# A state-space mixer, a feed-forward and linear attention on one core: y turned by feature tile from a buffer of its own, decay computed in place in four tiles, diagonals by chunk

## The chip, the cores and the metric

The kernel runs on one core of a Trainium2 chip. The core has a matrix engine (TensorE, PE in the profile, its weight loads PEld), a vector engine (VectorE, DVE), an activation engine (ScalarE, ACT), a general engine (GpSimd, POOL) and a queue processor (SyncE, SP). Each works through its own queue in order, and they wait for each other at semaphores. Tiles lie in an on-chip memory of 128 partitions (SBUF), matmul results in eight PSUM banks of 128 x 512 fp32 values. The metric is device time in microseconds of one execution.

## The reference

For 16 sequences of 512 tokens with 256 features the program computes four blocks, each with a layer norm in front and a residual add behind:

```python
x = x + mamba(layernorm(x), ...)      # L0_attn_a
x = x + ffn(layernorm(x), ...)        # "f"
x = x + attention(layernorm(x), ...)  # L0_attn_b, linear, causal, 16 heads
x = x + ffn(layernorm(x), ...)        # "g", same weights
```

The first block is a scan over time with 16 states per feature:

```python
x_in = x @ w_in;  dt_low, Bm, Cm = split(x_in @ w_x)
dt = softplus(dt_low @ w_dt + b_dt) * 0.099 + 0.001
A = -exp(A_log)
# at each token, for every feature d and state n:
h = exp(dt[d] * A[d, n]) * h + inp_term[n]     # inp_term sums dt * A * u over d, times Bm
y[d] = sum_n h[d, n] * Cm[n] + Dp[d] * x_in[d]
```

The feed-forward quantizes its inputs, its weights and its hidden layer to 4-bit floats in blocks of 16 and dequantizes them again: `fp4_linear(silu(fp4_linear(x, w_gate)) * fp4_linear(x, w_up), w_down)`. All is in fp32.

## The kernel before

A sequence b is one tile x of 128 x 4 x 256 (token in a chunk, chunk c, feature), which stays on the chip through all four blocks.

**Prologue** (`front`, L430, and `prologue`, L444). Mean and variance by `bn_stats` (L437), 1/sigma on GpSimd (L391). `to_features` (L408) turns x to 2 feature tiles of 128 x 512: for a layer norm it makes four diagonal matrices of 1/sigma (L414, one tile "diag" of four chunks with a single buffer) and multiplies each 128x128 piece of x by its diagonal on TensorE (L421), first the four chunks of feature tile k = 0 in one PSUM bank, then those of k = 1 in another, with a copy (L425) after each. From this come pz, tile "soft" (Abs, Tanh and Ln, L461 to L467), dt (L468, the last read of "soft"), which goes to DRAM as dd in eight DMAs (L473), C as cm (L478), u (L485) and the input term (L497).

**Mamba** (L501) has 16 steps, by feature half e (2), group j (4) and pair q0 (2). A step takes 16 features by two groups of eight, with the 16 states of eight features on 128 partitions.
- `spread` (L508) loads dt of these features from dd by DMA into a tile sp, 128 x 2 x 512, each row repeated for 16 states. sp has three buffers, and the load is asked for two steps ahead.
- `decay` (L518) computes bar = exp(dt A) as the square of the Exp of half the exponent: two Exp (L524) from sp into one of two constant tiles bar, then one Square in place (L527). It is written one step ahead of its scan. Column 0 of each bar stays zero, so that the scan starts anew there.
- A scan over 2 x 512 elements (L545) into h (three buffers), a product with cm (L549), and after every second step four matmuls (eight instructions, L555) that sum over the states into py. py is a single PSUM bank of its own pool (128 x 512, all of one half e); the half opens with a matmul by the diagonal of Dp (two instructions, L541) and ends with a copy to yT (L562).
- yT holds both halves (128 x 2 x 512) and has the tag "soft", with one buffer: it takes turns with the prologue's "soft" tile.
- When both halves are there, yT is turned back in eight 128x128 transposes (L571) into two banks, and `residual` (L374) adds each chunk of 128x256 to x on VectorE with its row sum (L377), followed by a Square on ScalarE that accumulates the squared distances from the mean (L381). These sums feed the next layer norm.

**Feed-forward** (`ffn`, L578) quantizes the normalized x, turns it, and then for each of the four chunks does gate and up matmuls (L599), silu (L605 to L607), quantization (L226 to L252), turning (L621, copied to hqT by L625) and the down matmul po (L634). **Attention** (L656) turns x with its 1/sigma by `to_features`, makes q and k (L671 to L679), and by chunk scores (four banks psc, masked to sm by L722), numerator and denominator, and the projection (L793).

Seven PSUM banks (pool `ps`, L73) serve all of this except py. A tile's buffer goes to the next tile of the same tag, in program order, when its last reader is done.

**Order.** The blocks are Python generators that yield weights; `weave` (L834) puts a piece of the next sequence's prologue after each step of mamba, and `by_turns` (L874) advances two generators in proportion to their weights. For sequence b the loop at L897 runs two such stages: mamba(b) with prologue(b+1) and the start of f(b) beside g(b−2) and the front of attention(b−1), then the chunks of f(b) beside the rest of attention(b−1). `some(new, FIRST)` cuts the first stage at a weight of 74. This is the order in which instructions are written. The framework then sets the order on each engine itself: earlier-written work goes first, and later work is taken up where it is ready and the engine would be free. In the trace, early scans of mamba(b) therefore stand between instructions of f(b−1) and attention(b−2).

Of the kernel before, what the change touches and what calls it, by code (L numbers as in the profile page):

```python
# [17 lines left out]
P = 128  # L18
# [14 lines left out]
def kernel(  # L33
# [31 lines left out]
    NBAR = 2  # L65
    NSP = 3
# [91 lines left out]
    for t in vpads:  # L158
        nc.gpsimd.memset(t, 0.0)

# [213 lines left out]
    def residual(xt, c, add, stats):  # L374
# [5 lines left out]
        )  # L380
        nc.scalar.activation(  # L381
# [26 lines left out]
    def to_features(pool, t, name, rstd=None):  # L408

        tT = pool.tile([P, ND, S], F32, tag="tT", name=f"tT_{name}", bufs=1)  # L410
        if rstd is not None:
            diag = small.tile([P, NC, P], F32, tag="diag", name=f"diag_{name}", bufs=1)
            for c in range(NC):
                nc.scalar.activation(diag[:, c, :], ident, AF.Copy, scale=rstd[:, c : c + 1])  # L414
        for k in range(ND):
            pt = bank(f"pt_{name}_{k}")
            for c in range(NC):
                if rstd is None:
                    nc.tensor.transpose(pt[:, ts(c, P)], t[:, c, ts(k, P)], ident)
                else:  # L420
                    nc.tensor.matmul(  # L421
                        pt[:, ts(c, P)], t[:, c, ts(k, P)], diag[:, c, :],
                        start=True, stop=True,
                    )
            nc.scalar.copy(tT[:, k, :], pt)  # L425
        return tT
# [74 lines left out]
    def mamba(b, xt):  # L501
# [5 lines left out]

        def spread(e, j, q0):  # L508

            sp = one.tile([P, 2, S], F32, tag="sp", name=f"sp_{b}_{e}_{j}_{q0}", bufs=NSP)  # L510
            src = dd[e, q0 // 2, j * G8 : (j + 1) * G8].rearrange("i q t -> i (q t)")
            nc.sync.dma_start(
                sp.rearrange("p q t -> p (q t)"),
                src.unsqueeze(0).to_broadcast([NS, G8, 2 * S]),
            )
            return sp

        def decay(sp, e, j, q0):  # L518

            bar = bars[state["bar"] % NBAR]  # L520
            state["bar"] += 1
            for i in range(2):
                g = 16 * e + 4 * (q0 + i) + j
                nc.scalar.activation(  # L524
                    bar[:, i, 1:S], sp[:, i, 1:S], AF.Exp, scale=a_col[:, g : g + 1]
# [5 lines left out]
        sps = [spread(*steps[at]) for at in range(NSP - 1)]  # L531
        ahead = decay(sps[0], *steps[0])
        for at, (e, j, q0) in enumerate(steps):
            bar = ahead
            if at + NSP - 1 < len(steps):
                sps.append(spread(*steps[at + NSP - 1]))
            if at + 1 < len(steps):
                ahead = decay(sps[at + 1], *steps[at + 1])
            if j == 0 and q0 == 0:
# [398 lines left out]
```

## Time and profile before

| | |
|---|---|
| median of 3 runs | 3023.27 us (3021.46 to 3023.94) |
| the profiled execution | 3014.09 us, span 3012.4 us |
| busy: TensorE, VectorE, ScalarE, GpSimd | 82%, 81%, 50%, 5% of the span |
| mean granted TensorE clock | 0.915 |
| L545 scans, 256 | 581.0 us, 2281 ns each |
| L549 products, 256 | 308.5 us, 1208 ns each |
| L524 Exps, 512 | 352.1 us, 716 ns each; idle before them 392.0 us |
| L527 Squares, 256 | 269.1 us, 1051 ns each |
| DMA of sp, 256 of 512 KB | 4.6 us to landing |

The profile is of one execution; times in views are microseconds from the span's start. A line of instructions gives its start, duration, engine, line of the kernel, operation and tiles (out<-in), and in brackets how long the engine had been idle and what ended that. A line of waits gives who waited for whom, the total, how many times, and the longest. The chain lists the work that ended last, step by step. Busy matmul time is modelled, so a full TensorE is not TensorE at its peak. From the fourth sequence on the first scans (L545) of sequences follow each other at 177.4 to 181 us.

### The profile page before, as it was taken

The numbers are of one execution on the slowest core, as the hardware profiler recorded it, in microseconds if no ns is written. First come the engines' busy times: TensorE is split into PE (matmuls) and PEld (weight loads), VectorE is DVE, ScalarE is ACT, GpSimd is POOL, SyncE is SP. The second block draws the span as 40 slices with busy tenths as digits, with TensorE's granted clock in tenths as the row PEclk, the third lists the DMA queues.
The fourth block names the chain that finished last, engine by engine and source line by source line (L and its number), as shares of the span: only waits on it lengthen the run. The fifth ranks groups of instructions, "written<-read, shape, count | busy, mean of one in ns | idle before, by whom it ended". The sixth has DMA issues, their size and how long they took to land.

```text
span 3012.4 us, 34256 instructions
## 1 busy us (share of the span) xinstructions
PE 2463.3 (82%) x12907; PEld 1464.3 (49%) x12907; DVE 2451.0 (81%) x3545; ACT 1507.3 (50%) x2846; POOL 144.7 (5%) x169
## 2 busy tenths in 40 slices
PE   6576898979888797888979788787878879787897
PEld 3142544545455454545545454454545545454654
DVE  7969679697897969889796987979698787987565
ACT  5746264554545555454555546455554645543222
POOL 2000000000000000000000000000000000000000
PEclk8787897998999899999999999899999989998988
DMA  5513012031231313112131311213122120310000
GB/s 140 133 42 98 21 44 76 22 91 36 54 80 29 79 34 91 36 49 77 32 80 36 83 44 49 70 28 84 37 78 54 46 74 22 84 35 1 8 1 14
DMA packets 64377, 165.27 MB, mean 55 GB/s; under 512 B 8434, under 2 KB 26836, under 8 KB 64212
## 3 DMA queue, kind: packets, MB, share of 16 engines
q1 hardware_dynamic: 62592, 162.03, 20.6%
q8 instruction: 101, 1.65, 0.2%
q10 hardware_dynamic: 1620, 1.06, 0.1%
q14 instruction: 64, 0.52, 0.1%
HBM read 146.28 MB, written 16.78 MB: 54 GB/s over the span
## 4 chain that ended last, share of the span: by engine, by line
DVE 49%; PE 31%; ACT 10%; issue 6%; POOL 2%; DMA 0%; DVEq 0%; SPq 0%; ACTq 0%; POOLq 0%
DVE h L545 13%; PE po_f L634 7%; DVE h L549 4%; PE pg_f L599 3%; PE pu_f L599 3%; PE po_g L634 3%; DVE sm L722 2%; DVE v_g L250 2%; DVE v_f L250 2%; DVE v_f L251 2%; DVE v_f L244 2%; DVE v_g L251 2%; PE pz L452 2%; PE py L555 2%; DVE h_g L252 1%
## 5 line engine op out<-in xcount | busy, mean ns | idle before, releaser
L545 DVE TENSOR_TENSOR_SCAN h<-bar,inp 128x1024 f32<-128x1024 f32 x256 | 581.0, 2281 | 7.7 <-ACT bar L527 3.3
L524 ACT ACTIVATE bar<-sp,a_col 128x511 f32<-128x511 f32 x512 | 352.1, 716 | 392.0 <-DVE h L545 384.5
L555 PE MATMUL py<-h,red 128*32 128x512 f32 x1024 | 280.8, 691 | 155.7 <-DVE h L549 155.7
L549 DVE TENSOR_TENSOR h<-h,cm 128x1024 f32<-128x1024 f32 x256 | 308.5, 1208 | 1.3
L634 PE MATMUL po_f<-wdT,hqT_f 128*128 128x256 f32 (+1 forms) x768 | 220.4, 434 | 68.6 <-ACT hqT_f L625 68.6
L527 ACT ACTIVATE bar<-bar 128x1022 f32<-128x1022 f32 x256 | 269.1, 1051 | 4.4
L634 PE MATMUL po_g<-wdT,hqT_g 128*128 128x256 f32 (+1 forms) x768 | 208.8, 416 | 22.5 <-ACT hqT_g L625 22.5
L634 PEld LDWEIGHTS po_f<-wdT,hqT_f 128*128 128x128 f32 (+1 forms) x768 | 152.7, 213 | 139.7 <-ACT hqT_f L625 93.1
L634 PEld LDWEIGHTS po_g<-wdT,hqT_g 128*128 128x128 f32 (+1 forms) x768 | 145.0, 202 | 96.7 <-ACT hqT_g L625 36.9
L599 PE MATMUL pg_f<-wgT,tT_f 128*128 128x352 f32 x512 | 182.1, 479 | 0.2 <-ACT tT_f L425 0.2
L599 PE MATMUL pg_g<-wgT,tT_g 128*128 128x352 f32 x512 | 179.1, 472 | 0.1
L679 DVE SCALAR_TENSOR_TENSOR qk<-ep 128x512 f32<-128x512 f32 x64 | 44.0, 688 | 164.1 <-ACT ep L678 164.1
L599 PE MATMUL pu_g<-wuT,tT_g 128*128 128x352 f32 x512 | 177.1, 464 | 0.0
L599 PE MATMUL pu_f<-wuT,tT_f 128*128 128x352 f32 x512 | 173.4, 461 | 0.0
L722 DVE TENSOR_TENSOR sm<-psc,causal 128x512 f32<-128x512 f32 x256 | 161.9, 679 | 13.3 <-PE psc L715 9.0
L621 PE MATMUL pt_h_g<-ident,h_g 128*128 128x128 f32 (+1 forms) x384 | 69.7, 322 | 117.8 <-DVE h_g L252 117.8
L555 PEld LDWEIGHTS py<-h,red 128*32 128x32 f32 x1024 | 35.3, 113 | 264.3 <-DVE h L549 210.0
L248 ACT ACTIVATE big_f<-v_f 128x704 bf16<-128x704 f32 (+1 forms) x80 | 67.2, 840 | 146.1 <-DVE v_f L244 146.1
L599 PEld LDWEIGHTS pg_g<-wgT,tT_g 128*128 128x128 f32 x512 | 95.3, 192 | 80.2 <-issue 41.4
L621 PEld LDWEIGHTS pt_h_g<-ident,h_g 128*128 128x128 f32 (+1 forms) x384 | 47.6, 155 | 178.3 <-DVE h_g L252 141.6
L606 DVE SCALAR_TENSOR_TENSOR h_f<-h_f,pg_f 128x352 f32<-128x352 f32 x128 | 66.1, 517 | 76.8 <-ACT h_f L605 76.8
L599 PEld LDWEIGHTS pu_g<-wuT,tT_g 128*128 128x128 f32 x512 | 97.1, 192 | 63.3 <-issue 12.6
(236 smaller groups left out, 4814.8 us busy)
## 6 DMA issues: line engine op xcount, KB each, us to landing
sp<-dd SPq DMA_DIRECT2D x256, 512.0 KB, 4.6
x<-in_L_attn_a_x_dram SPq DMA_DIRECT2D x16, 512.0 KB, 4.3
dd<-dt SPq DMA_DIRECT2D x128, 64.0 KB, 1.7
out_dram<-x SPq DMA_DIRECT2D x16, 512.0 KB, 3.5
w_qkv_sb<-in_L_attn_b_W_attn_dram ACTq DMA_DIRECT2D x1, 768.0 KB, 7.1
raw_d<-in_L_ffn_w_down_dram SPq DMA_DIRECT2D x1, 704.0 KB
raw_g<-in_L_ffn_w_gate_dram SPq DMA_DIRECT2D x1, 640.0 KB, 7.0
raw_u<-in_L_ffn_w_up_dram SPq DMA_DIRECT2D x1, 640.0 KB, 6.2
```

What stands on the lines that cost most here:

```text
L248: nc.scalar.activation(big, v, AF.Abs, scale=STEP)
L250: nc.vector.scalar_tensor_tensor(v, big, FLOOR, v, ALU.max, ALU.subtract)
L251: nc.vector.scalar_tensor_tensor(v, big, FLOOR, v, ALU.max, ALU.subtract)
L524: nc.scalar.activation(bar[:, i, 1:S], sp[:, i, 1:S], AF.Exp, scale=a_col[:, g : g + 1])
L527: nc.scalar.activation(bar[:, :, 1:S], bar[:, :, 1:S], AF.Square)
L545: nc.vector.tensor_tensor_scan(h.rearrange("p i t -> p (i t)"), bar.rearrange("p i t -> p (i t)"), inp.rearrange("p i t -> p (i t)"), 0.0, ...
L549: nc.vector.tensor_tensor(h, h, cm.unsqueeze(1).to_broadcast([P, 2, S]), ALU.mult)
L555: nc.tensor.matmul(py[32 * q : 32 * q + 32, :], red[:, j, :], (h0, h)[q // 2][:, q % 2, :], start=False, stop=(j == 3),)
L599: nc.tensor.matmul(pw[:, :HF], xqT[:, k, ts(c, P)], wT[:, k, cols], start=(k == 0), stop=(k == ND - 1),)
L621: nc.tensor.transpose(pt[:rows, ts(r - r0, P)], h[:, r * P : r * P + rows], ident)
L634: nc.tensor.matmul(po[:, :D], hqT[:rows, r, :], wdT[:rows, r, :], start=(r == 0), stop=(r == NR - 1),)
L722: nc.vector.tensor_tensor(t, psc[g].rearrange("p (s t) -> p s t", t=P), causal.unsqueeze(1).to_broadcast([P, NH // 4, P]), ALU.mult,)
```

## The change

- **y by feature tile.** At the end of each half e, py is copied to a tile yT of 128 x 512 that has a tag and a buffer of its own. Its four 128x128 pieces are turned into one bank and added to the feature half of x at once, on VectorE, as four instructions of 128x128 with partial row sums in `halves`. After the second half the two partial sums are added (128 x 4), and the four Squares follow (`distances`, split off from `residual`). The end of mamba yields 2 in place of 1.7.
- **Decay in place.** There are four bar tiles in place of two, and no sp. `spread` loads dt straight into bar, without column 0 (511 elements per row, two rows per partition), and Exp works in place. The load for step at + 3 is written after the decay of step at + 1, before the scan of step at.
- **Diagonals by chunk.** `to_features` with 1/sigma makes one 128x128 diagonal per chunk (tag "diag", two buffers, the pool's default) and uses it for both feature tiles, so two banks are filled side by side and copied at the end.

```diff
--- before.py
+++ after.py
@@ -62,8 +62,7 @@
     HF = FF // 2
     HB = P // HD
     G8 = P // NS
-    NBAR = 2
-    NSP = 3
+    NBAR = 4
     NV = 2
     NSM = 6
     DT_MIN, DT_MAX = 0.001, 0.1
@@ -378,6 +378,9 @@
             xt[:, c, :], add, 1.0, xt[:, c, :], ALU.mult, ALU.add,
             accum_out=sums[:, c : c + 1],
         )
+        distances(xt, c, sums, dist)
+
+    def distances(xt, c, sums, dist):
         nc.scalar.activation(
             squares, xt[:, c, :], AF.Square, bias=sums[:, c : c + 1], scale=-float(D),
             accum_out=dist[:, c : c + 1],
@@ -408,21 +411,23 @@
     def to_features(pool, t, name, rstd=None):
 
         tT = pool.tile([P, ND, S], F32, tag="tT", name=f"tT_{name}", bufs=1)
-        if rstd is not None:
-            diag = small.tile([P, NC, P], F32, tag="diag", name=f"diag_{name}", bufs=1)
-            for c in range(NC):
-                nc.scalar.activation(diag[:, c, :], ident, AF.Copy, scale=rstd[:, c : c + 1])
+        if rstd is None:
+            for k in range(ND):
+                pt = bank(f"pt_{name}_{k}")
+                for c in range(NC):
+                    nc.tensor.transpose(pt[:, ts(c, P)], t[:, c, ts(k, P)], ident)
+                nc.scalar.copy(tT[:, k, :], pt)
+            return tT
+        pts = [bank(f"pt_{name}_{k}") for k in range(ND)]
+        for c in range(NC):
+            diag = small.tile([P, P], F32, tag="diag", name=f"diag_{name}_{c}")
+            nc.scalar.activation(diag, ident, AF.Copy, scale=rstd[:, c : c + 1])
+            for k in range(ND):
+                nc.tensor.matmul(
+                    pts[k][:, ts(c, P)], t[:, c, ts(k, P)], diag, start=True, stop=True
+                )
         for k in range(ND):
-            pt = bank(f"pt_{name}_{k}")
-            for c in range(NC):
-                if rstd is None:
-                    nc.tensor.transpose(pt[:, ts(c, P)], t[:, c, ts(k, P)], ident)
-                else:
-                    nc.tensor.matmul(
-                        pt[:, ts(c, P)], t[:, c, ts(k, P)], diag[:, c, :],
-                        start=True, stop=True,
-                    )
-            nc.scalar.copy(tT[:, k, :], pt)
+            nc.scalar.copy(tT[:, k, :], pts[k])
         return tT
 
 
@@ -505,37 +510,35 @@
         nc.scalar.copy(inp[:, 0, :], term)
         nc.gpsimd.tensor_copy(inp[:, 1, :], term)
 
+        halves = small.tile([P, ND, NC], F32, tag="halves", name=f"halves_{b}")
+
         def spread(e, j, q0):
-
-            sp = one.tile([P, 2, S], F32, tag="sp", name=f"sp_{b}_{e}_{j}_{q0}", bufs=NSP)
-            src = dd[e, q0 // 2, j * G8 : (j + 1) * G8].rearrange("i q t -> i (q t)")
-            nc.sync.dma_start(
-                sp.rearrange("p q t -> p (q t)"),
-                src.unsqueeze(0).to_broadcast([NS, G8, 2 * S]),
-            )
-            return sp
-
-        def decay(sp, e, j, q0):
 
             bar = bars[state["bar"] % NBAR]
             state["bar"] += 1
+            src = dd[e, q0 // 2, j * G8 : (j + 1) * G8, :, 1:S]
+            nc.sync.dma_start(bar[:, :, 1:S], src.unsqueeze(0).to_broadcast([NS, G8, 2, S - 1]))
+            return bar
+
+        def decay(bar, e, j, q0):
+
             for i in range(2):
                 g = 16 * e + 4 * (q0 + i) + j
                 nc.scalar.activation(
-                    bar[:, i, 1:S], sp[:, i, 1:S], AF.Exp, scale=a_col[:, g : g + 1]
+                    bar[:, i, 1:S], bar[:, i, 1:S], AF.Exp, scale=a_col[:, g : g + 1]
                 )
             nc.scalar.activation(bar[:, :, 1:S], bar[:, :, 1:S], AF.Square)
             return bar
 
         steps = [(e, j, q0) for e in range(ND) for j in range(4) for q0 in (0, 2)]
-        sps = [spread(*steps[at]) for at in range(NSP - 1)]
+        sps = [spread(*steps[at]) for at in range(NBAR - 1)]
         ahead = decay(sps[0], *steps[0])
         for at, (e, j, q0) in enumerate(steps):
             bar = ahead
-            if at + NSP - 1 < len(steps):
-                sps.append(spread(*steps[at + NSP - 1]))
             if at + 1 < len(steps):
                 ahead = decay(sps[at + 1], *steps[at + 1])
+            if at + NBAR - 1 < len(steps):
+                sps.append(spread(*steps[at + NBAR - 1]))
             if j == 0 and q0 == 0:
                 py = ps_y.tile([P, S], F32, tag="y", name=f"py_{b}_{e}")
                 nc.tensor.matmul(py, d_diag[:, e], u[:, e, :], start=True, stop=False)
@@ -557,23 +560,25 @@
                         start=False, stop=(j == 3),
                     )
             if j == 3 and q0 == 2:
-                if e == 0:
-                    yT = one.tile([P, ND, S], F32, tag="soft", name=f"yT_{b}")
-                nc.scalar.copy(yT[:, e, :], py)
+
+                yT = one.tile([P, S], F32, tag="yT", name=f"yT_{b}_{e}")
+                nc.scalar.copy(yT, py)
+                pt = bank(f"pt_y_{b}_{e}")
+                for c in range(NC):
+                    nc.tensor.transpose(pt[:, ts(c, P)], yT[:, ts(c, P)], ident)
+                for c in range(NC):
+                    xc = xt[:, c, ts(e, P)]
+                    nc.vector.scalar_tensor_tensor(
+                        xc, pt[:, ts(c, P)], 1.0, xc, ALU.mult, ALU.add,
+                        accum_out=halves[:, e, c : c + 1],
+                    )
             yield 3.5
 
-
-        stats["f", b] = summed(0, f"f{b}")
-        for c in range(0, NC, 2):
-            pt = bank(f"pt_y_{b}_{c}")
-            for i in range(2):
-                for e in range(ND):
-                    nc.tensor.transpose(
-                        pt[:, ts(i * ND + e, P)], yT[:, e, ts(c + i, P)], ident
-                    )
-            for i in range(2):
-                residual(xt, c + i, pt[:, ts(i, D)], stats["f", b])
-        yield 1.7
+        stats["f", b] = sums, dist = summed(0, f"f{b}")
+        nc.vector.tensor_tensor(sums, halves[:, 0, :], halves[:, 1, :], ALU.add)
+        for c in range(NC):
+            distances(xt, c, sums, dist)
+        yield 2
 
     def ffn(i, nm, b, xt):
         act = acts[i]
```

## The prediction

> **What bounds the kernel now.** I read first the page's busy times, then a window view of one period, then the timeline where one engine stands idle, then waits and chain.
>
> ```profile
> PE 2463.3 (82%) x12907; PEld 1464.3 (49%) x12907; DVE 2451.0 (81%) x3545; ACT 1507.3 (50%) x2846; POOL 144.7 (5%) x169
> ```
>
> VectorE (DVE) and TensorE (PE) stand level at about four fifths, so an average cannot say which of them limits. The scans of a sequence (L545) come round every 177.4 us in the middle of the run; one such period in three windows (span, then busy time and count of each engine), then L545 alone (busy time and count on VectorE):
>
> ```profile
> core 0: us, PE busy (x) PEld busy (x) DVE busy (x) ACT busy (x) POOL busy (x), PEclk, DMA share, GB/s
> 1161.20:1233.20 72.00, 51.67 (x316) 32.58 (x316) 69.75 (x102) 36.26 (x70) 3.59 (x4) 0.88 0.31 81
> 1233.20:1311.20 78.00, 72.70 (x398) 44.30 (x398) 53.75 (x89) 40.68 (x81) 3.78 (x4) 1.00 0.11 28
> 1311.20:1338.60 27.40, 23.11 (x91) 11.43 (x89) 26.92 (x30) 16.09 (x27) 0.61 (x1) 1.00 0.29 77
> ```
>
> ```profile
> 1161.20:1251.20 90.00, 23.43 (x11) 0.91 0.29 76
> 1251.20:1312.20 61.00, 1.47 (x1) 1.00 0.07 19
> 1312.20:1338.60 26.40, 11.40 (x5) 1.00 0.30 79
> ```
>
> The first window is VectorE's (2.3 us idle of 72), the second TensorE's (5.3 idle of 78, while VectorE idles 24.3), the third VectorE's again (0.5 idle). And no scan starts for 61 us in the middle: eleven of sixteen run early, five wait until 1312. What holds them is in the timeline:
>
> ```profile
> 1293.80 1.23 DVE L468 SCALAR_TENSOR_TENSOR dt<-soft,dt 128x1024 f32<-128x1024 f32 x1 [1.06 <-ACT soft L467]
> ...
> 1296.58 0.59 ACT L562 COPY yT<-py 128x512 f32<-128x512 f32 x1
> ...
> 1298.89 1.02 PE L541 MATMUL py<-u,d_diag 128*128 128x512 f32 x2
> ...
> 1312.61 2.28 DVE L545 TENSOR_TENSOR_SCAN h<-bar,inp 128x1024 f32<-128x1024 f32 x1
> ```
>
> The last py matmul of the first half ended at 1243.7, but its copy yT shares the buffer "soft" with the next sequence's prologue and must let that tile through first (last read: L468). Until then py, a single PSUM bank, cannot take the second half; the three h buffers fill with steps 8 to 10, and step 11's scan has nowhere to write. Last, the waits and a piece of the chain:
>
> ```profile
> ACT bar L524 <- DVE h L545: 384.5, 193, 7.2
> ```
>
> ```profile
> 1225.25 2.21 DVE h L545
> 1227.46 0.02 issue
> 1227.48 0.72 ACT bar L524
> 1228.20 0.48 ACT hqT_f L625
> ```
>
> ScalarE (ACT) runs its queue in order. With two bar buffers an Exp (L524) waits for the scan two steps back, and the feed-forward's copies behind it wait as well: here hqT_f, which po_f's matmuls need, comes after an Exp that stood behind a scan.
>
> **The change part by part.** The profiled execution took 3014.1 us (span 3012.4, 1.7 around it); the median of the runs is 3023.3, so I add 9.2 at the end. Costs are per period; there are 14, since sequences 1 to 14 all show the hole.
>
> *A buffer of its own for yT.* The copy no longer waits for "soft"; py is free at about 1245, and steps 11 to 15 become ready one after the other in the second window. They are 5 scans of 2.28 and 5 products (L549) of 1.22 = 17.5 us that now lie in the third, where VectorE is full. Of the window's 24.3 idle us some 20 lie after 1245; into them go perhaps 13: one gap alone is 10.0 us (before L679, 1280.99 to 1290.99), the others are 1 to 1.7 us, which hold a product but not a scan. −13, between 0 and −17.5. A scan put into a 1.5 us gap holds up what comes next by some 0.8; two or three of these: +2 (0 to +6). With the scans go their matmuls, into a window where TensorE is nearly full. A half has 32 py instructions and two for d_diag; the timeline has eight of py in 1.06 (at 1309.72) and the two in 1.02, so 4 × 1.06 + 1.02 = 5.3 us (9.4 if they run in fours, which take 1.05 at 1314.40). The window has 5.3 idle, of which I let rather more than half be of use: +2 (0 to +9.4). What is late next: yT of the second half has the same single buffer and waits until the first half is turned (a bank for pt_y, L571, which low-priority work gets around 1276 at the latest, as pt_m did). That is after most of the scans, and no scan waits for it.
>
> *Turning and adding by feature tile.* Eight transposes before and after. Four additions of 128x256 (0.414 each, from PSUM) become eight of 128x128. From 0.414 at 256 and 0.520 at 352 (L606, also from PSUM) an element costs 1.1 ns, so 0.27 each: 2.2 against 1.7. Four more accumulator reads of 0.077 and one 128x4 sum (0.17, by L399): together +1.0, between +0.3 (at the 0.219 of a 128x64 operation from PSUM, L821) and +2.1 (at 0.414). VectorE would be held in order behind scan, py, copy and turn if the additions stood straight after the last product. For the additions of before the profile has 1.8 us of idle in all 16 sequences, so other work is put ahead of them: 0; without that cover 3 us per half (py 1.05, copy 0.59, half of the eight turns' 1.0, and the hand-overs). The squares (L381) now start only after all additions: four of 0.5 behind, but four turns fewer before: 0.
>
> *Four bars, filled by DMA and overwritten by Exp.* Same Exps and Squares. The wait for the scan goes: 26 us per period stand in ScalarE's queue, but only two places lie on the chain as above (1225 and 1243). Each could give at most 2.9; other releasers come soon after: −2 (0 to −5.8). In its place Exp waits for the DMA, and the DMA, at the head of SP's queue, for the scan three steps before the step it loads. Behind it on SP stand the next x load, the eight dd writes and the output. Three steps of at least 3.5 us are 10.5; issue 0.5, landing 4.6, Exp and Square 2.5 come to 7.6: in time. The rows are now 2044 bytes in place of 4096. The x load has rows of 1024 bytes and lands as fast:
>
> ```profile
> sp<-dd SPq DMA_DIRECT2D x256, 512.0 KB, 4.6
> x<-in_L_attn_a_x_dram SPq DMA_DIRECT2D x16, 512.0 KB, 4.3
> ```
>
> so 0; at the longest landing of sp (8.0) the step would be 0.5 late, eight times: +4 at most. The dd writes were issued at 1295 and are needed around 1316, so a few us behind a waiting load cost nothing. [...]
>
> *Diagonals by chunk.* Eight ScalarE instructions of 0.387 as before. The third now waits until both matmuls of the first are done, and both banks are held from the first chunk to the last copy. At 1280.6 to 1283.8 that adds about 0.2, twice: +0.5 (−0.3 to +3, if ScalarE is busy at each hand-over).
>
> *Sum.* −13 + 2 + 2 + 1 − 2 + 0.5 = −9.5 per period; 14 × 9.5 = 133. 3014.1 − 133 = 2881; with 9.2, **2890**. Sequence 0 has no hole, and sequence 15 a short one: 0.
>
> **The rivals.**
> *Full packing.* All 17.5 land in idle time, both chain places give 2, and the matmuls and the added work (2 + 1 + 0.5) stay: −17.5 − 4 + 3.5 = −18, × 14 = −252, 2771. VectorE's 150.4 busy of 177.4 leaves room; that its idle time is in pieces speaks against.
> *TensorE keeps the third window.* It is busy 23.1 there, so the window may shrink by only 4.3 whatever leaves VectorE. With the added work (+1.5) and some collision, −2 × 14 = −28: 2995. For it: the second window is TensorE's too. Against: py's matmuls leave the third window with the scans.
> *Slower: banks.* pt_y of the first half and pt_m, which now takes two banks at once, ask while attention's scores want four of the seven. A bank lent to pt_y is held for about 2 us (four turns 0.6, four additions 1.2). If in each of the four chunks attention and the feed-forward wait once for such a bank, that is 8 × 2 = 16 against the 9.5 won: +6.5 × 14 = 91, 3114; with six waits +2.5, 3058. It decides from five waits in a period. Against: attention's products (L722) wait 9.0 us for PE in the whole run now; for: pt_m's diagonals were ready at 1211 and its matmuls ran at 1276.
> *It doesn't do what it says* (the hole has another cause) would leave about 3020; the copy's place 1.5 us after L468's end in period after period leaves it little.
>
> **How the numbers follow.** Forecast 0.52 (2790 to 2960), full packing 0.10, TensorE's window or no effect 0.20, banks 0.18. The range is 2780 to 3060: it leaves out most of full packing and the worse half of banks. A change of 0.2%, 6 us, is about what measurement can tell from none. Faster: 0.52 + 0.10 + 0.16 of the third = 0.78; same: 0.03 of the third and 0.02 of the fourth; slower: 0.17, the rest of these.
>
> **What would show it.** Right: no stretch of 61 us without scans, yT's first copy some 50 us earlier, the period near 168 and VectorE's idle time in it near 17 (27 less 9.5); "bar <- h" all but gone from the waits, with no "bar <- DMA" in its place; sp's landing for bar near 4.6; 0.27 for the additions. Wrong: scans early but a third window still 27 long (TensorE), waits of sm, pg or pt_m for a bank, or Exps behind landings of 8 and more.

## The result and the profile after

The changed kernel takes 3048.58 us (median; 3041.72 to 3052.38) against 3023.22 (four runs of each): **1.0082 of the time before, 95% interval 1.0064 to 1.0101**. I had forecast 2890, a gain, and had put 0.17 on a loss. The profiled execution took 3041.72 us (span 3040.0).

The page's busy times, and L548 (the scan) alone in one period of 180.8 us, from the first scan of a sequence on (span, then busy time and count on VectorE):

```profile
PE 2544.4 (84%) x12907; PEld 1482.9 (49%) x12907; DVE 2459.3 (81%) x3689; ACT 1489.1 (49%) x2846; POOL 174.7 (6%) x171
```

```profile
core 0: us, DVE busy (x), PEclk, DMA share, GB/s
1154.84:1269.30 114.46, 36.08 (x16) 0.88 0.26 65
1269.30:1335.61 66.31, 0.00 (x0) 0.97 0.18 40
```

The stretch of 61 us without scans in the middle is gone: all sixteen scans run in the first 114 us. But the period has not become shorter. The same period with all engines (span, then busy time and count of each, granted clock, DMA share):

```profile
1154.84:1269.30 114.46, 95.95 (x516) 54.88 (x517) 105.90 (x148) 50.17 (x96) 5.79 (x5) 0.88 0.26 65
1269.30:1290.90 21.60, 20.30 (x145) 12.70 (x144) 17.03 (x36) 6.71 (x20) 1.41 (x2) 1.00 0.00 1
1290.90:1314.80 23.90, 22.12 (x83) 13.54 (x82) 8.88 (x14) 17.20 (x30) 1.95 (x1) 0.93 0.05 12
1314.80:1335.61 20.81, 19.24 (x62) 10.24 (x60) 19.32 (x34) 17.69 (x31) 1.21 (x1) 1.00 0.50 113
```

VectorE idles 8.6 us in the 114.5 with scans, and 15.0 in the 23.9 from 1290.90 on. Its idle time has moved to where no scan is left, and it is not less: 29.0 us per period against 27.0 before (means over eight and seven periods). What starts at 1292 is the prologue of the next sequence, and the next scan waits for it. The timeline shows what lies between (start, duration, engine and line):

```profile
1229.45 0.58 ACT L565 COPY yT<-py 128x512 f32<-128x512 f32 x1 [0.54 <-PE py L558]
...
1315.89 0.60 PE L568 MATMUL pt_y<-ident,yT 128*128 128x128 f32 x4
...
1316.58 0.59 ACT L565 COPY yT<-py 128x512 f32<-128x512 f32 x1
...
1347.30 0.66 PE L568 MATMUL pt_y<-ident,yT 128*128 128x128 f32 x4
```

The first half's copy runs 74.6 us into the period; before it ran 61 us later (+135.7 on the mean), behind the prologue's "soft". The turn (pt_y) of that copy, however, runs 86 us after it, at +161, the second half is copied only then, and its turn follows at +192, although the last scan ended at +114. The profile names no releaser for the turn. x is whole only after that, and f(b) starts from x.

**Where the time went, as a sum.** In every profile the prologue's pt_m follows within 0.1 us on f's last po_f, as here in the changed kernel:

```profile
1289.09 3.05 PE L639 MATMUL po_f<-wdT,hqT_f 128*128 128x256 f32 x12 [0.46 <-ACT hqT_f L630]
1292.07 2.70 PE L426 MATMUL pt_m<-diag_m,x 128*128 128x128 f32 x16
```

So two periods can be cut into five parts without a gap, from the first scan of sequence b over its y, f(b) and the prologue of b + 2 to the first scan of b + 2. Means over sequences 4 to 13, in us:

| from, to | before | after |
|---|---|---|
| first scan, last addition of y | 185.2 | 195.6 |
| last addition, first xn_f (f's normalised input) | 3.4 | 13.0 |
| xn_f, end of f's last po_f | 105.3 | 108.5 |
| pt_m, end of the prologue's dt | 18.2 | 19.7 |
| dt, first scan of b + 2 | 43.6 | 23.6 |
| sum = two periods | 355.7 | 360.4 |

The last row but one is the gain: 20.0 us, 10.0 per period, because five late scans of the sequence before no longer stand between dt and the next first scan. The first two rows took 10.4 + 9.6 back, the others 4.7. That is +2.35 per period, some 33 us over 14; the spans differ by 27.6. The sum says where the time lies; what causes it is for the experiments.

The second row in the timeline, after and then before, from y's last addition to xn_f:

```profile
1350.55 0.28 DVE L571 SCALAR_TENSOR_TENSOR x<-pt_y,x 128x128 f32<-128x128 f32 x1
...
1356.75 0.16 DVE L578 TENSOR_TENSOR sum_f<-halves 128x4 f32<-128x4 f32 x1
...
1359.21 0.51 ACT L384 ACTIVATE squares<-x,sum_f 128x256 bf16<-128x256 f32 x1
...
1361.17 2.28 DVE L548 TENSOR_TENSOR_SCAN h<-bar,inp 128x1024 f32<-128x1024 f32 x1
...
1361.34 2.91 POOL L394 TENSOR_TENSOR rstd_f<-var_f,neg_half 128x4 f32<-128x4 f32 x1 [26.40 <-DVE var_f L392]
1364.29 0.41 DVE L405 TENSOR_SCALAR xn_f<-x,mean_f,rstd_f 128x256 f32<-128x256 f32 x1 [0.52 <-POOL rstd_f L394]
```

```profile
1168.09 0.41 DVE L377 SCALAR_TENSOR_TENSOR x<-pt_y,x 128x256 f32<-128x256 f32 x1
...
1170.77 1.01 POOL L391 TENSOR_TENSOR rstd_f<-var_f,neg_half 128x4 f32<-128x4 f32 x1 [11.83 <-DVE var_f L389]
...
1171.86 0.36 DVE L402 TENSOR_SCALAR xn_f<-x,mean_f,rstd_f 128x256 f32<-128x256 f32 x1
```

Before, the first Square started at 1167.94, 0.57 us before the last addition ended. After, the 128x4 sum of the halves must come first and stands 5.9 us behind other work of VectorE; the four Squares follow in a row, and GpSimd's rstd takes 2.91 beside a scan.

Waits (engine and line, whom they waited for, us in total, times, longest), and the chain in one period:

```profile
ACT bar L527 <- DMA bar<-dd: 321.8, 143, 6.7
PEld py L558 <- DVE h L552: 264.0, 81, 10.2
ACT squares L384 <- DVE x L377: 253.9, 88, 8.5
ACT big_f L248 <- DVE v_f L244: 208.4, 62, 6.2
PE py L558 <- DVE h L552: 191.1, 67, 10.0
```

```profile
1163.60 2.21 DVE h L548
1165.90 4.42 DMA bar<-dd
1170.40 0.72 ACT bar L527
1171.12 0.69 ACT big_g L248
...
1206.73 6.09 DMA bar<-dd
...
1244.92 4.79 DMA bar<-dd
```

Exp's wait for the scan (384.5 us before) is all but gone, and in its place stands a wait of 321.8 us for the load; a load lies on the chain three times in this period, 15.3 us. Each load itself is as fast as I took it:

```profile
bar<-dd SPq DMA_DIRECT2D x256, 511.0 KB, 4.8
x<-in_L_attn_a_x_dram SPq DMA_DIRECT2D x16, 512.0 KB, 3.9
```

### The profile page after: what moved, and what is told of

It is laid out like the page before. It is cut to its first block, busy times and chain, and to the rows that moved or that the text cites. A ratio compares the mean times of both kernels' runs of the same rounds, so it can differ in the third digit from the quotient of the medians.

```text
span 3040.0 us, 34253 instructions
## 1 busy us (share of the span) xinstructions
PE 2544.4 (84%) x12907; PEld 1482.9 (49%) x12907; DVE 2459.3 (81%) x3689; ACT 1489.1 (49%) x2846; POOL 174.7 (6%) x171
## 4 chain that ended last, share of the span: by engine, by line
DVE 45%; PE 26%; ACT 14%; DMA 6%; issue 5%; POOL 4%; SPq 0%; DVEq 0%; ACTq 0%; POOLq 0%
DVE h L548 12%; DMA bar<-dd 6%; DVE h L552 5%; PE po_f L639 4%; DVE sm L727 3%; ACT bar L527 2%; PE py L558 2%; DVE v_g L250 2%; DVE amax_f L230 2%; PE pro L798 2%; PE pg_f L604 2%; DVE v_g L251 2%; PE po_g L639 2%; PE pu_f L604 2%; DVE v_f L251 1%
## 5 line engine op out<-in xcount | busy, mean ns | idle before, releaser
L548 DVE TENSOR_TENSOR_SCAN h<-bar,inp 128x1024 f32<-128x1024 f32 x256 | 578.0, 2276 | 6.3 <-ACT bar L530 4.6
L527 ACT ACTIVATE bar<-bar,a_col 128x511 f32<-128x511 f32 x512 | 347.4, 714 | 366.8 <-DMA bar<-dd 321.8
L558 PE MATMUL py<-h,red 128*32 128x512 f32 x1024 | 340.7, 697 | 191.3 <-DVE h L552 191.1
L639 PE MATMUL po_g<-wdT,hqT_g 128*128 128x256 f32 (+1 forms) x768 | 218.3, 431 | 38.8 <-ACT hqT_g L630 38.5
L639 PE MATMUL po_f<-wdT,hqT_f 128*128 128x256 f32 (+1 forms) x768 | 207.1, 414 | 25.7 <-ACT hqT_f L630 25.7
L558 PEld LDWEIGHTS py<-h,red 128*32 128x32 f32 x1024 | 43.7, 114 | 334.0 <-DVE h L552 264.0
L639 PEld LDWEIGHTS po_f<-wdT,hqT_f 128*128 128x128 f32 (+1 forms) x768 | 142.8, 199 | 99.5 <-ACT hqT_f L630 40.5
L684 DVE SCALAR_TENSOR_TENSOR qk<-ep 128x512 f32<-128x512 f32 x64 | 44.0, 687 | 180.2 <-ACT ep L683 180.2
L604 PE MATMUL pg_g<-wgT,tT_g 128*128 128x352 f32 x512 | 177.7, 469 | 0.1
L604 PE MATMUL pu_f<-wuT,tT_f 128*128 128x352 f32 x512 | 175.5, 466 | 2.3 <-DVE sm L727 2.3
L604 PEld LDWEIGHTS pu_f<-wuT,tT_f 128*128 128x128 f32 x512 | 99.2, 194 | 59.7 <-issue 4.3
L604 PEld LDWEIGHTS pg_f<-wgT,tT_f 128*128 128x128 f32 x512 | 95.1, 197 | 56.1 <-issue 13.8
L676 PE MATMUL pqk<-tT_a,w_qkv_sb 128*128 128x512 f32 x256 | 119.9, 594 | 0.5 <-ACT tT_a L430 0.5
```

The source lines that it names most:

```text
L527: nc.scalar.activation(bar[:, i, 1:S], bar[:, i, 1:S], AF.Exp, scale=a_col[:, g : g + 1])
L548: nc.vector.tensor_tensor_scan(h.rearrange("p i t -> p (i t)"), bar.rearrange("p i t -> p (i t)"), inp.rearrange("p i t -> p (i t)"), 0.0, ...
L558: nc.tensor.matmul(py[32 * q : 32 * q + 32, :], red[:, j, :], (h0, h)[q // 2][:, q % 2, :], start=False, stop=(j == 3),)
L604: nc.tensor.matmul(pw[:, :HF], xqT[:, k, ts(c, P)], wT[:, k, cols], start=(k == 0), stop=(k == ND - 1),)
L639: nc.tensor.matmul(po[:, :D], hqT[:rows, r, :], wdT[:rows, r, :], start=(r == 0), stop=(r == NR - 1),)
L676: nc.tensor.matmul(pz, w_qkv_sb[:, k, ts(je, P)], xnT[:, k, :], start=(k == 0), stop=(k == ND - 1),)
```

## The experiments

All ratios are to the kernel before, run on the same chip, with 95% intervals. The first theory (A) put the loss on the four bars and their loads, its rival (B) on the y part. Theory C, on the early turn of y and its bank, and E, on TensorE's queue, came later. D stands for two things: in tile_late's expectation for the additions by feature tile and the late Squares, in after_turn_py's for the four bars. The table has what every run gave; "last scan" (its end) and "y added" are us after the sequence's first scan, means over sequences 4 to 13 as above.

| kernel | ratio | last scan | y added | period |
|---|---|---|---|---|
| before | 1 | 174.9 | 185.2 | 177.9 |
| before_34 | 0.9999 [0.9989, 1.0009] | 175.9 | 187.3 | 179.2 |
| before_36 | 0.9983 [0.9973, 0.9992] | 176.9 | 190.3 | 178.8 |
| diag_only | 1.0039 [1.0025, 1.0053] | 175.7 | 186.0 | 178.7 |
| decay_only | 1.0174 [1.0159, 1.0189] | 179.7 | 192.2 | 182.2 |
| after | 1.0082 [1.0064, 1.0101] | 114.0 | 195.6 | 180.2 |
| after_nudge (3.4) | 0.9879 [0.9858, 0.9900] | 137.2 | 186.5 | 175.2 |
| after_36 | 1.0298 [1.0282, 1.0313] | 107.7 | 207.2 | 185.5 |
| py_later | 1.0070 [1.0054, 1.0087] | 113.5 | 194.7 | 179.5 |
| y_diag | 1.0219 [1.0189, 1.0250] | 128.1 | 199.7 | 183.7 |
| early_two | 1.0229 [1.0212, 1.0246] | 129.5 | 200.8 | 184.7 |
| tile_late | 1.0087 [1.0072, 1.0102] | 113.7 | 203.3 | 180.9 |
| own_first | 0.9822 [0.9798, 0.9845] | 128.1 | 196.8 | 175.5 |
| own_first_b3 | 0.9811 [0.9796, 0.9827] | 127.0 | 195.8 | 174.4 |
| own_first_36 | 1.0456 [1.0439, 1.0474] | 129.3 | 213.1 | 191.2 |
| own_bank | 0.9968 [0.9952, 0.9985] | 140.1 | 178.7 | 179.3 |
| turn_in_py | 0.9798 [0.9773, 0.9823] | 129.7 | 137.9 | 175.6 |
| after_turn_py | 0.9718 [0.9680, 0.9755] | 127.6 | 135.8 | 173.8 |
| whole_turn_py | 0.9719 [0.9694, 0.9744] | 130.8 | 158.1 | 174.1 |
| turn_py_36 | 0.9859 [0.9841, 0.9877] | 101.2 | 122.7 | 177.7 |

**One part alone.** decay_only is the kernel before with four bars filled and overwritten in place; diag_only has the diagonals by chunk alone.

```diff
 decay_only
-    NBAR = 2
-    NSP = 3
+    NBAR = 4
...
-                    bar[:, i, 1:S], sp[:, i, 1:S], AF.Exp, scale=a_col[:, g : g + 1]
+                    bar[:, i, 1:S], bar[:, i, 1:S], AF.Exp, scale=a_col[:, g : g + 1]
 diag_only
-            diag = small.tile([P, NC, P], F32, tag="diag", name=f"diag_{name}", bufs=1)
+            diag = small.tile([P, P], F32, tag="diag", name=f"diag_{name}_{c}")
```

> The kernel before with the decay's part alone: four bars filled by DMA, Exp in place, no sp. Theory A (the new wait of ScalarE for the DMA into bar, 322 us in the profile after, three places of 4.4 to 6.1 us on the chain of a period, costs what the moved scans won): slower than before by 30 to 80 us, 3050 to 3100, with waits of bar for DMA over 200 us. Theory B (the scans were moved for nothing: the period is set by the next sequence's prologue and by the turning of y that waits for a bank): 3010 to 3030, since the hole in the scans stays as it was.

> The kernel before with the diagonals by chunk alone. Both theories: 3018 to 3035, that is 0 to +12 us (my term was +0.5 per period, 7 in all). More than +20 us would make the two banks held side by side a cause of its own.

In the kernel before, the four bars cost 51.7 us (3065.84 against 3014.16), 3.7 per period; that is within theory A's 3050 to 3100. The hole is still there, since nothing else was changed (in the sequence that starts at 1183.1 no scan starts from +81 to +158). The wait for the load is there, and DMA is 9% of the chain:

```profile
ACT bar L519 <- DMA bar<-dd: 293.1, 111, 6.1
```

The diagonals cost 11 us, 0.8 per period.

**The change without the four bars.** y_diag is the changed kernel with sp and two bars again; early_two is y_diag with the second half of y in soft's buffer.

```diff
 y_diag
-    NBAR = 4
+    NBAR = 2
+    NSP = 3
 early_two (to y_diag)
-                yT = one.tile([P, S], F32, tag="yT", name=f"yT_{b}_{e}")
+                if e == 0:
+                    yT = one.tile([P, S], F32, tag="yT", name=f"yT_{b}")
+                else:
+                    yT = one.tile([P, ND, S], F32, tag="soft", name=f"yT1_{b}")[:, 1, :]
```

> The changed kernel with the decay undone (sp and two bars again), so y by feature tile and diagonals by chunk. Theory A: 2890 to 2970, the hole of 60 us gone and no wait for DMA. Theory B: 3020 to 3050, all scans early, no scan in the last third of the period, VectorE idle there.

> As y_diag, with the early turn of the first half, but the second half is copied to the buffer of soft, so that it does not wait until the first is turned. Theory C with the single buffer at its core: 0.980 to 0.995 of before. Theory C with the bank or the place of the turn at its core: 1.01 to 1.03, as y_diag.

Theory A falls as the explanation of the whole: without the four bars the kernel is not faster but 14 thousandths slower than the changed one, slower than B forecast too (3077.87 against 3020 to 3050). The part that costs 17 thousandths in the kernel before shows no loss here; but 14 thousandths is also a size that the written order alone can move, as the last runs show. early_two says that it isn't the second half's wait for the single yT buffer either: another buffer for it moves nothing (1.0229 against 1.0219).

**The buffer without the early turn.** own_first gives only the first half of y a buffer of its own; the second goes to soft's as before, and both are turned and added at the end in four additions of 128x256. tile_late turns at the end too, but by feature tile, with the sum of the halves and the late Squares. own_first_b3 has three bars and two sp.

```diff
 own_first (to diag_only)
-                    yT = one.tile([P, ND, S], F32, tag="soft", name=f"yT_{b}")
-                nc.scalar.copy(yT[:, e, :], py)
+                    y0 = one.tile([P, S], F32, tag="yT", name=f"yT0_{b}")
+                    nc.scalar.copy(y0, py)
+                else:
+                    y1 = one.tile([P, ND, S], F32, tag="soft", name=f"yT1_{b}")
+                    nc.scalar.copy(y1[:, 1, :], py)
 own_first_b3 (to own_first)
-    NBAR = 2
-    NSP = 3
+    NBAR = 3
+    NSP = 2
```

> The kernel before with the diagonals by chunk and only one thing of y's part: the first half of y goes to a buffer of its own, the second to the buffer of soft, turned and added at the end by chunk as before. Theory A: the hole is gone as in y_diag, 2890 to 2970. Theory B with the bank at its core (the early turning of the first half holds a bank and y's single buffer, so the second half is turned late): this one is faster than y_diag by 15 us or more, since it turns nothing early; without the bank, the two are equal within 10 us.

> y added by feature tile (eight additions of 128x128, partial sums, four Squares behind), but both halves turned and added after the last step, with the first half in its own buffer and the second in that of soft; sp and two bars, diagonals by chunk. Theory C (the early turn is what costs: its bank is asked for after step 7, and it is turned in the middle of the other blocks): within 15 us of own_first (ratio 0.982), so 0.980 to 0.988 of before. Theory D (the additions by feature tile and the late Squares cost): within 15 us of y_diag, 1.015 to 1.025.

> own_first with three bars and two sp in place of two and three (the same memory). ScalarE's wait of Exp for the scan (306 us in own_first) should fall below 150 us, since the scan is that of three steps back and sp still loads ahead. If that wait is on the chain: 10 to 40 us faster than own_first, 0.969 to 0.979 of before. If the wait only moves to the landing of sp: equal within 10 us or slower, with waits of bar for DMA over 100 us.

own_first is faster than both kernels (0.9822). It copies the first half at +74, about when the changed kernel does, and from the last addition to xn_f it needs 5.3 us where tile_late needs 9.0 and the changed kernel 13.0. Its 2957 us lie in A's range as well as in B's. tile_late's 1.0087 lies between the ranges of C and D and decides for neither. A third bar gives nothing: Exp's wait for the scan falls from 306.1 only to 220.1 us, not below 150, and the time stays. Taken alone these runs say that the buffer pays and that the turn and the additions by feature tile lose it again; the last runs below show how far that holds.

**Another bank for the turn.** pt_y takes py's bank, which is free at that moment, in place of one of the seven shared ones: in y_diag (turn_in_py), in the changed kernel itself (after_turn_py), and there with the diagonals of a sequence in one tile again (whole_turn_py). own_bank gives pt_y a bank of its own and leaves six to be shared.

```diff
 turn_in_py, after_turn_py
-                pt = bank(f"pt_y_{b}_{e}")
+                pt = ps_y.tile([P, S], F32, tag="y", name=f"pt_y_{b}_{e}")
 own_bank
-    ps = ctx.enter_context(tc.tile_pool(name="ps", bufs=7, space=PSUM))
+    ps = ctx.enter_context(tc.tile_pool(name="ps", bufs=6, space=PSUM))
+    ps_t = ctx.enter_context(tc.tile_pool(name="ps_t", bufs=1, space=PSUM))
...
-                pt = bank(f"pt_y_{b}_{e}")
+                pt = ps_t.tile([P, S], F32, tag="t", name=f"pt_y_{b}_{e}")
```

> As y_diag, but the turned y goes to the bank of py (pool ps_y) and not to one of the seven banks of pool ps; so the turn need not wait for one of these, and the second half of py waits until the first half is added. If the wait for a bank of ps is what costs: 0.975 to 0.99 of before, first additions some 5 us after the copy of y in place of 88. If it is the work that is moved into the chain of attention and feed-forward: 1.00 to 1.02, with the additions early.

> The changed kernel with one line other: the turn of y (pt_y) is written to the bank of py and no longer to one of the seven shared banks. Theory C (the time is lost because the shared banks are handed out in the order written, so that the early turn gets its bank 86 us after its copy, and the half's additions, the f stage and the next prologue come late): ratio to the kernel before 0.965 to 0.985, the first half turned within 5 us of its copy (about +80 of the period), pt_m of the next sequence at +133 or earlier, a period of 174 to 177. Theory D (the time is lost to the four bars: Exp of the step four on waits for its load in ScalarE's queue, whatever bank the turn has): 0.995 or more, with the ScalarE wait for a load (322 us) unchanged. Both at once: ScalarE's wait for the load stays above 250 us and the ratio lies between, at or above turn_in_py's 0.980.

> The changed kernel with a bank for pt_y alone and six shared banks in place of seven. Theory C says that any bank outside the shared order serves: first half turned within 5 us of its copy, ratio 0.965 to 0.99. A rival within it (the seven banks are themselves short, and the turn in py's bank won only because it costs the others none): six banks make the f and attention stages late, ratio 1.0 or more although the turn comes early.

> after_turn_py with the diagonals of a sequence in one tile, as before the change. If the diagonals by chunk cost what they did alone (1.0039), this run is 0.003 to 0.005 below after_turn_py (8 to 14 us). If they cost something only where VectorE was late anyway, within 0.002 of it; if more (both halves' banks are claimed at once), 0.006 or more below.

With this one line the changed kernel goes from 1.0082 to 0.9718, and y_diag from 1.0219 to 0.9798. In the timeline of after_turn_py (a sequence that starts at 1111.9) copy, turn and addition now follow each other directly:

```profile
1180.96 0.57 ACT L565 COPY yT<-py 128x512 f32<-128x512 f32 x1
...
1181.58 0.66 PE L568 MATMUL pt_y<-ident,yT 128*128 128x128 f32 x4 [1.98 <-ACT yT L565]
...
1185.52 0.29 DVE L571 SCALAR_TENSOR_TENSOR x<-pt_y,x 128x128 f32<-128x128 f32 x1
```

0.6 us from copy to turn, where it was 86; y is whole 8 us after the last scan, where it was 82. The wait of ScalarE for loads is even longer, 350.4 us for 321.8, and the kernel gains all the same. In own_bank the turns come 14 us (first half) and 18.5 us (second) after their copies, where the theory had 5, and the ratio is 0.9968, between the theory's and the rival's numbers: an outside bank brings the turn forward, and a seventh shared bank seems to be worth something too. The diagonals' price of 4 thousandths isn't found again here (0.9719 and 0.9718).

**The planner's number.** The last runs change the weight that each step of the scan loop yields, 3.5, to 3.4 or 3.6. No work changes, only the order in which the blocks are written. (The first expectation calls it the last step's number; the edit stands in the loop and holds for all sixteen.)

```diff
-            yield 3.5
+            yield 3.4
```

> The changed kernel with a number of the planner changed alone: the last step of a scan loop is given 3.4 in place of 3.5, which may reorder a few instructions and changes no work. If the times of these kernels follow mechanisms, within 0.003 of the changed kernel's 1.0082. If it moves by 0.01 or more, the order that the planner happens to write is worth as much as the parts told apart here, and differences of that size between kernels show no mechanism by themselves.

> The kernel before with 3.4 in place of 3.5 as the planner's number for each step of the scan loop; the work is the same. If the change itself did the harm, the kernel before is steady: 0.997 to 1.003. If the written order is worth 2% in these kernels whatever their design, it moves by 0.01 or more in either direction. Theory E (TensorE's in-order wait for h at py's matmuls decides): whatever the ratio is, it goes with that wait, which was 156 us at 1.000 and changes by about 100 us for 0.02.

> The kernel before with 3.6. Same expectations as with 3.4: 0.997 to 1.003 if the loss belongs to the change, a move of 0.01 or more if it belongs to the order; Theory E: the ratio follows TensorE's wait for h at py's matmuls (156 us at 1.000, 0.02 per 100 us).

> The changed kernel with 3.6. If 3.5 was an unlucky order, this falls near 3.4's 0.988 (0.98 to 0.995); if 3.4 was a lucky one, it stays at 1.003 to 1.015. Theory E: TensorE's wait for h at py's matmuls below 120 us in the first case, above 170 in the second.

> The changed kernel with the turn of y in py's bank, and 3.6, the number at which the changed kernel itself was slowest (1.0298). Theory C (the shared banks are where the written order decides when y is added; outside of them the additions come about 10 us after the last scan, whatever the number): 0.963 to 0.982, y added by +140, and nothing of the 0.022 by which the changed kernel grew from 3.5 to 3.6. If the gain of 0.036 at 3.5 was a lucky order: 0.985 to 1.02.

> The kernel with an own buffer for the first half alone (turn and additions at the end, as before the change) with 3.6. If the early turn and the additions by feature tile make the changed kernel depend on the planner's number, this one stays at 0.977 to 0.988 (0.9822 with 3.5). If any own buffer does, since the scans packed early leave VectorE without work while f's banks are waited for, it rises as the changed kernel did: 0.995 to 1.02.

With 3.4 the weights ahead of f's chunks come to 73.6 in the changed kernel (16 × 3.4, mamba's end 2, the prologue's 8.0, f's 2.2 and 7) and 73.3 in the one before, so f's turn (1) is still written before the cut at 74; with 3.5 and 3.6 it isn't. The kernel before doesn't care: 0.9999, 1, 0.9983. The changed one goes from 0.9879 over 1.0082 to 1.0298, with the same parts. So its 0.8% is one draw out of a range of 4%, and the three numbers' mean, 1.0086, is not far from it. own_first's gain was such a draw as well: 0.9822 becomes 1.0456. With 3.6 its first half is copied at +72 as with 3.5, its second at 1363.92 of a sequence that starts at 1197.4, and then:

```profile
1363.92 0.60 ACT L567 COPY yT<-py 128x512 f32<-128x512 f32 x1
...
1405.69 1.04 PE L576 MATMUL pt_y<-ident,yT 128*128 128x128 f32 x8
...
1407.90 0.42 DVE L377 SCALAR_TENSOR_TENSOR x<-pt_y,x 128x256 f32<-128x256 f32 x1
```

42 us between copy and turn, y whole at +213, a period of 191. That wait is hardly longer than with 3.5 (40 us); what grew is the second half's copy (+166 for +154) and f (117.5 us from xn_f to the last po_f, for 104.7). So here the order did its harm mostly elsewhere. What lasts is the bank: at 3.5 it is worth 0.0364 (1.0082 to 0.9718), at 3.6 0.0439 (1.0298 to 0.9859), in y_diag 0.0421. But turn_py_36 misses theory C's range (0.963 to 0.982) and lies in its rival's (0.985 to 1.02): with the turn in py's bank too, the time rises by 0.0141 from 3.5 to 3.6. y is not what rose, it is added at +123, earlier than with 3.5. So the gain by the bank holds in three pairs of kernels, and part of the dependence on the order stays with the other bank (0.0141, for 0.0216 with the shared ones). after_36 (1.0298) and own_first_36 (1.0456) lie above every range that they had been given. With 3.4 ScalarE waits longer for its loads than with 3.5, and the kernel is 2% faster:

```profile
ACT bar L527 <- DMA bar<-dd: 398.5, 160, 7.1
```

**py's matmuls later.** Theory E was TensorE's in-order wait for h at py's matmuls. py_later writes them one scan later.

```diff
             if q0 == 0:
                 h0 = h
+                if j > 0:
+                    reduce(py, j - 1, *pair)
             else:
-                for q in range(4):
-                    nc.tensor.matmul(
...
+                pair = (h0, h)
+            if j == 3 and q0 == 2:
+                reduce(py, j, *pair)
```

> The changed kernel with the py matmuls of each pair of scans written one scan later, so that TensorE meets them when h is more likely done. Theory E (TensorE stands in order at py's matmuls, 191 us, and the work behind them is late): that wait falls below 120 us and the ratio to 0.975 to 0.995. If that wait is a mere companion of another delay: 1.003 or more, with the wait shifted to other work. A cost on the other side: h is held one scan longer, so with three h buffers a scan may wait for py's matmuls, up to 1.02.

The wait stayed at 191.3 us, against 191.1: the framework puts these matmuls where it did before, so the edit did nothing and its run tells nothing. E falls by other runs, before_34 at 0.9999 and after_36 at 1.0298:

```profile
PE py L555 <- DVE h L549: 289.2, 73, 6.0
...
PE py L558 <- DVE h L552: 112.2, 66, 10.3
```

**Three of these runs, cut as the table above.** In after_nudge y is whole at +186.5, about as before the change, and the second row stays long (12.4 us): two periods take 350.3, 5.4 less than before. In own_first y is as late as in the changed kernel (+196.8) and the second row is short (5.3): 350.9. So neither loss alone took the gain away; the changed kernel has both. In after_turn_py y is whole 60 us earlier than in the changed kernel, but from xn_f to the last po_f it then takes 160.9 us in place of 108.5, and two periods are 12.7 shorter: past that, something else holds f. The runs differ in their order too, so this is an account and not a test.

## Why the prediction was wrong, point by point

**What bounds the kernel, and the hole: right.** The hole came from the soft buffer; the copy now runs 61 us earlier, the stretch of 61 us without scans is gone from the middle, and "bar <- h" is all but gone. But one of 66 us now stands at the end of the period.

**A buffer for yT, −13 + 2 + 2: right in size.** dt to first scan fell by 20.0 us in two periods, 10.0 per period, against −9 for the three terms together. That is the whole of the gain, and it was there.

**"What is late next … no scan waits for it": the step that failed.** I dated the first half's turn to 1276 at the latest, some 115 us into the period, and asked only which scan would wait. It ran at +161, the second at +192. No scan waits for it, but x does: y whole → f(b) → its last po_f, with pt_m right behind → the prologue of b + 2 → the next scan but one period. The additions, which before came 10 us after the last scan, now come 82 us after it and 10.4 later in the period: +5.2 per period where I had put 0. That the bank is the reason, and that another one pays, is shown by the one-line runs (0.0364, 0.0421 and 0.0439); why the shared banks reach pt_y so late is not: the profile names no releaser for the turn.

**"The squares now start only after all additions: 0": wrong.** From the last addition to xn_f 13.0 us in place of 3.4, +4.8 per period. I counted four Squares behind against four turns fewer, and left out that the 128x4 sum waits in VectorE's order behind other work (5.5 us on the mean) and that rstd meets a scan (2.91 in place of 1.01). The additions themselves were right: 0.28 each (median) for 0.27.

**The four bars, load in time: wrong premise, size at the end of the range.** Landing was 4.8, with rows of 2044 bytes in a DMA of 511 KB, for 4.6 with rows of 4096 before; the row of x (4.3 with rows of 1024) decided rightly. But "three steps of at least 3.5 us" doesn't hold once scans run in pairs (at +37 and +39, +47 and +50, +88 and +90), and so the load is late: 321.8 us of waits. Alone the part cost 3.7 per period, near the +4 at most that I gave. In the changed kernel it isn't the whole loss: without it the time is longer (y_diag), and with it and another bank the kernel gains (after_turn_py).

**Diagonals, +0.5:** 0.8 alone, inside the bounds.

**The rivals.** "Slower: banks" had 0.18 and named the resource, with 3058 to 3114 for a time of 3048.6; the victim was another: not attention and the feed-forward waiting for a bank lent to pt_y, but pt_y waiting for theirs. That its figures lie close to the time is luck. "TensorE keeps the third window" is not what happened: what remained is a window in which VectorE idles.

**What no step held.** I took the written order as fixed and as good after the change as before. With the soft buffer the late scans were held to a place where they filled the prologue's time, and the period hardly moved with the order (0.9983 to 1); without it the time moves over 4%. That the soft buffer is what kept the kernel before steady fits this, but no run shows it by itself. A forecast of the sign needed that order, not the costs.

## What to carry to other kernels

When a wait goes, follow the value that it delayed through every buffer up to the next iteration, and ask of each link who takes it up next; a shared pool in the path (here seven banks, handed on in the written order) can hold an early request as long as the wait did, and a buffer that is free at that point can take it out of that order (here 0.6 us from copy to turn, for 86). Before a difference of one or two per cent is put down to a part, move the planner's numbers a little in both kernels: a kernel that was steady can become one whose time is a draw.

## What the runs showed of the hardware

**TensorE's clock.** Where TensorE stood for h for 6.23 us, the work behind took nearly twice as long until 1194 (start, duration; count at the end of each line):

```profile
1175.27 0.88 PE L626 MATMUL pt_h_g<-ident,h_g 128*128 128x128 f32 x6 [1.67 <-DVE h_g L252]
...
1188.83 1.91 PE L558 MATMUL py<-h,red 128*32 128x512 f32 x2 [6.23 <-DVE h L552]
1190.84 1.54 PE L626 MATMUL pt_h_g<-ident,h_g 128*128 128x128 f32 x6
...
1198.60 1.05 PE L558 MATMUL py<-h,red 128*32 128x512 f32 x4 [1.27 <-DVE h L552]
...
1226.31 1.19 PE L782 MATMUL pkv<-vpad,kt 128*128 128x128 f32 x4 [2.77 <-DVE sm L727]
```

Six turns took 1.54 in place of 0.88, and two py matmuls 1.91 where four took 1.05 at 1198.60. The granted clock was half from 1184.20 to 1194.44, and once more from 1225.16 to 1235.40 (span, PE busy and count, granted clock, DMA share, GB/s):

```profile
1180.79:1184.20 3.41, 1.80 (x7) 1.00 0.40 79
1184.20:1194.44 10.24, 5.52 (x11) 0.50 0.15 44
...
1221.75:1225.16 3.41, 1.42 (x4) 1.00 0.00 0
1225.16:1235.40 10.24, 8.37 (x18) 0.50 0.00 0
```

The halving at 1184.20 came 1.6 us after TensorE stopped at 1182.59, and the full clock was back 5.6 us after the work resumed at 1188.83; at the halving of 1225.16 the longest pause around it was 2.77 us. In this trace the clock changes on a grid of 3.41 us. Of its 79 halvings 77 follow a stretch of the grid in which TensorE was busy for 54% or less, and none of the 638 stretches at full clock that were not followed by one had it busy for under 46%. So here it halved after stretches about half idle, as far as the modelled busy times tell.

TensorE's busy time rose from 2463.3 to 2544.4 us for the same 12,907 matmuls. It worked 421.4 us at half clock, 349.6 before; if work slows there as the six turns did (1.54 for 0.88), the 71.8 more cost some 31 us (an estimate from these numbers), under half of the rise. The rest is not explained here. I had given such stalls no price beyond their length.

**GpSimd beside a scan.** The 128x4 rstd took 2.9 us in 14 of its 64 runs after, and in all 14 a scan of VectorE ran beside it; in the 50 without a scan it took 1.0 to 2.0. Before, 3 of 64 met a scan: two took 2.9 and 3.0, the third 1.0. What tells them apart is who came first: the 16 slow ones of both kernels started 0.1 to 0.2 us after a scan and ended 0.8 us after its end, the quick one started 0.3 us before its scan. Why is not shown here.
